# Moving sixteen element-wise sums and products of a mixture-of-experts stage from GpSimd to VectorE

## The chip, the cores and the metric

The kernel runs on one core of a Trainium2 chip. A core has five engines that work at once and tell each other of finished work through semaphores: TensorE (PE in the profile; its weight loads are listed as PEld), VectorE (DVE), ScalarE (ACT), GpSimd (POOL) and SyncE (SP), which in this kernel issues most DMAs. GpSimd also issues the indirect DMAs (gathers and scatters by a list of rows). The metric is the device time of one execution in microseconds (us); of several runs the median is taken.

## The reference, cut to what matters

There is one block of a transformer with four batches of 512 tokens of width 256. First comes attention with 16 heads, then a mixture of eight experts of which every token uses two. Both halves are normalized, modulated by a small vector per batch, and added back through a gate.

```python
h = _layernorm(x) * (1 + ca) + sa
x = x + ga * attention(h)                      # 16 heads of 128, causal
h = _layernorm(x) * (1 + cb) + sb
down   = h @ down_w + down_b                   # 256 -> 128
probs  = softmax(h @ router_w + router_b - cost)
top 2 of 8 experts, gate = softmax(of the two probabilities)
out    = sum over the two experts e of gate * (gelu(gelu(down) @ w1[e] + b1[e]) @ w2[e] + b2[e])
out   += 0.1 * (gelu(gelu(down) @ shared_w1 + shared_b1) @ shared_w2 + shared_b2)
y      = out @ up_w + up_b + gelu(h) @ core_w + core_b
x      = x + gb * y
```

Everything is float32. The experts have hidden widths of 128 to 512.

## The kernel before, in words

**Layout.** Tokens stand on the 128 partitions; a batch is four tiles of 128 tokens by 256 columns (`xs[b]`, in the trace `x`). Two neighbouring tiles are handled as one operand of 128 x 512.

**Attention stage.** A loop over 64 heads, four heads of one batch at a time, runs from the start to about 630 us of the span. Three heads are still on their way when it ends; their last products are made between the first steps of the next stage. When four heads of a batch are summed in PSUM (`po`), `project_out` multiplies by the gate on VectorE (L626, `tmp`) and adds to `x` (the call of `on_pool` in its last lines).

**Mixture stage** (`all_ffn`, from about 620 us to the end). For each batch, in this order:

- `second_norm` normalizes, makes the modulated rows, and calls `down` (L665 on TensorE, L673 and L674 on VectorE), `route` (a run of small VectorE instructions, L696 to L741, which finds the two experts of each token and their gates) and `to_rows`.
- `to_rows` calls `place` (L814 and L817 on TensorE from the tile `mine`, L825 to L841 on VectorE: the row of each token in a table sorted by expert) and `bring` (L857: eight indirect DMAs on GpSimd that scatter the tokens into `table`).
- `Experts.get` (L963) loads the sorted rows through SyncE, `turn` (L973) transposes them on VectorE (`full_s`). `Chunks` then runs 20 chunks of 128 hidden units per batch: first product (L1025, `ph_s`), activation on ScalarE (L1033, `hid_s`), second product three chunks later (L983, `acc_s`). After each pair of experts VectorE takes the sum out (L993, `y_s`) and SyncE stores it in `given` (L1001).
- `take` (trace line L594, tile `taken`): eight indirect DMAs on GpSimd that gather each token's two expert rows from `given`. `gated` weighs the two (L1086 on ScalarE, L1087 on VectorE).
- `core` (L1156), `combine` (L1105 and L1113 on TensorE, L1122 on ScalarE) and `up` (L1170) make the output; `up` multiplies by the gate on VectorE (L1178) and adds `x`. The last three batches do this after all chunks; the first does it among the chunks of the third.
- `gate_bias`, once per batch: `gbias`, the two output biases' sum times the gate (128 x 256), is added to both halves of `x`. This is done ahead of the output.

**What sets the order.** In this stage TensorE, VectorE, ScalarE and SyncE run their instructions in the order in which the program emits them. `PLAN` says at which of the 80 chunks each side step is emitted. GpSimd is left to the scheduler, except that `on_pool` ties every GpSimd instruction behind the one before (`pool_order`), so that its instructions keep the order of emission too. Each engine's queue is served strictly in turn: an instruction that waits holds back all that stand behind it on its engine. All calls through `on_pool` show as L594 in the profile.

GpSimd's queue in the mixture stage, in order: scatter of batch 1; two adds into `x` of batch 3 (last heads); `gbias` of batches 0 and 1 and their four adds; two small steps of batch 3's norm; scatter of batch 2; gather of batch 0; scatter of batch 3; two adds of batch 0's outputs; `gbias` of batch 2 and its first add; two DMAs of batch 1's gather; second add of batch 2; the other six DMAs; `gbias` of batch 3 and its two adds; gather of batch 2; gather of batch 3.

Of the kernel before, what the change touches and what calls it, by code (L numbers as in the profile page):

```python
# [16 lines left out]
ALU = mybir.AluOpType  # L17
# [94 lines left out]
def adaln_attention_moe_kernel(  # L112
# [14 lines left out]
    nc = tc.nc  # L127
# [476 lines left out]
    def project_out(b: int, h: int, z):  # L604


        g, j = h // HG, h % HG
        if j == 0:
            outs[b, g] = [
                psum.tile([P, 2, D], F32, tag=f"po{u}", name=f"po_{b}_{g}_{u}", bufs=1)  # L610
                for u in range(NT // 2)
            ]
        for u, po in enumerate(outs[b, g]):
            for t in range(2):
                tok = ts(2 * u + t, P)

                mm3(
                    po[:, t, :],
                    (z[0][:, tok], z[1][:, tok]),
                    part(wo_u[h // 2], (h % 2) * D, D),  # L620
                    j == 0 and t == 0,
                    j == HG - 1 and t == 1,
                )
            if j == HG - 1:
                tmp = work.tile([P, 2, D], F32, tag="tmp", name=f"tmp_{b}_{g}_{u}")
                nc.vector.tensor_tensor(tmp, po, pair(gate_a[b]), ALU.mult)  # L626
                xu = xs[b][:, 2 * u : 2 * u + 2, :]
                on_pool(nc.gpsimd.tensor_tensor, xu, xu, tmp, ALU.add)

# [506 lines left out]
    def gate_bias(b: int):  # L1138

        gbias = work.tile([P, D], F32, tag="vf", name=f"gbias_{b}", bufs=3)  # L1140
        on_pool(nc.gpsimd.tensor_tensor, gbias, rest_state["obias"], gate_b[b], ALU.mult)
        yield
        for u in range(NT // 2):
            xu = xs[b][:, 2 * u : 2 * u + 2, :]
            on_pool(nc.gpsimd.tensor_tensor, xu, xu, pair(gbias), ALU.add)
            yield

    pys: dict[tuple[int, int], bass.AP] = {}
# [15 lines left out]
    def up(b: int, u: int, last: bool = False, also: str = ""):  # L1164
        py = pys[b, u]
        y = work.tile([P, 2, D], F32, tag="tmp", name=f"y_{b}_{u}{also}")
        xu = xs[b][:, 2 * u : 2 * u + 2, :]
# [8 lines left out]
            )  # L1176
        if not last:
            nc.vector.tensor_tensor(y, py, pair(gate_b[b]), ALU.mult)  # L1178
            if also or b == 0:
                on_pool(nc.gpsimd.tensor_tensor, y, y, xu, ALU.add)  # L1180
            else:
                nc.vector.tensor_tensor(y, y, xu, ALU.add)
            stores.append((out[r0 : r0 + 2 * P, :].rearrange("(t p) d -> p t d", p=P), y))
            return
        for t in range(2):
# [553 lines left out]
```

## Time and profile before

| | us |
|---|---|
| median of 5 runs | 796.26 |
| lowest and highest | 792.53, 797.79 |
| the profiled execution | 796.48 |
| its span, first to last instruction | 794.8 |
| TensorE busy | 750.8 (94%) |
| VectorE busy | 541.0 (68%) |
| GpSimd busy | 470.4 (59%) |
| mean granted TensorE clock | 0.973 |

In a timeline each line has the start, the duration, the engine, the program's line, the operation, the tile written `<-` the tiles read, the shapes, and a count; brackets hold the idle time of the engine just before it and what ended this idle time. "remote" or "another core or an unknown queue" means that the profile can't name what ended it, and "issue" that it shows no wait that ended then. In a table by stage each row has the stretch of the span, its length, each engine's busy time with its instructions in brackets, the granted TensorE clock, the share of the DMA engines, and GB/s. The end of a matmul is modelled and not measured.

The sixteen instructions that the change touches take this time on GpSimd: eight adds of `gbias` to `x`, 10.1 us; four products `gbias`, 2.9 us; two adds of batch 0's outputs, 2.5 us; two adds of the last heads, 2.5 us.

### The profile page before, as it was taken

What the parts mean: (1) busy time and instruction counts of PE and PEld (TensorE: products, weight loads), DVE (VectorE), ACT (ScalarE), POOL (GpSimd) and SP (SyncE); (2) the same over time, 40 slices, a digit from 0 to 9 for tenths busy, and PEclk for the clock granted to TensorE, in tenths of its full rate; (3) what the DMA queues carried; (4) which work ended last, traced back from release to release, by engine and by line L of the source; (5) the groups of instructions that cost most, each with busy time, mean ns of one, the idle gap of its engine ahead of it and who ended that gap; (6) DMA issues with size and microseconds to landing.
All of it is one profiled execution on the core that took longest, in us unless ns stands there. A gap on an engine that the chain in (4) does not pass through costs nothing.

```text
span 794.8 us, 14400 instructions
## 1 busy us (share of the span) xinstructions
PE 750.8 (94%) x4641; PEld 679.0 (85%) x4641; DVE 541.0 (68%) x1753; ACT 470.8 (59%) x1180; POOL 470.4 (59%) x497
## 2 busy tenths in 40 slices
PE   8999999999999999999999999998998989478895
PEld 8899999999999999999999999997987879467784
DVE  6897887777777777777767777777785766133323
ACT  4668676776666677666667766665664436144430
POOL 4467657676655668675657786665467255634640
PEclk9999999999999999999999999999999999798997
DMA  7455455665566678776667756543567524352522
GB/s 254 134 178 193 128 166 147 178 200 147 143 177 186 166 212 227 209 189 184 180 166 197 216 152 179 161 141 112 152 188 187 129 54 100 73 113 72 125 87 73
DMA packets 111554, 124.68 MB, mean 157 GB/s; under 512 B 42592, under 2 KB 96624, under 8 KB 111472
## 3 DMA queue, kind: packets, MB, share of 16 engines
q1 hardware_dynamic: 109008, 119.47, 54.4%
q0 software_dynamic: 2048, 4.20, 1.8%
q8 instruction: 39, 0.64, 0.3%
q14 instruction: 43, 0.35, 0.1%
q10 hardware_dynamic: 416, 0.02, 0.0%
HBM read 64.92 MB, written 58.73 MB: 156 GB/s over the span
## 4 chain that ended last, share of the span: by engine, by line
PE 84%; DVE 7%; issue 3%; POOL 2%; another core or an unknown queue 1%; ACT 1%; DMA 1%; SPq 0%; DVEq 0%; ACTq 0%
PE ph_s L1025 4%; PE ps L139 4%; PE ps L138 4%; PE pz L139 4%; PE pz L140 4%; PE ps L140 4%; PE pz L138 4%; PE acc_s L983 4%; PE pv L140 4%; PE pv L139 4%; PE pv L138 4%; PE po L138 3%; PE po L140 3%; PE pk L139 3%; PE po L139 3%; PE pk L140 3%
## 5 line engine op out<-in xcount | busy, mean ns | idle before, releaser
L522 POOL TENSOR_SCALAR e<-e,inv 128x128 f32<-128x128 f32 (+3 forms) x256 | 137.4, 544 | 206.1 <-DVE inv L521 195.7
L517 ACT ACTIVATE e<-e,nmax 128x128 f32<-128x128 f32 (+3 forms) x256 | 144.0, 565 | 75.6 <-DVE nmax L507 73.9
L146 POOL TENSOR_TENSOR aT<-aT,aTh 128x1152 fp32r<-128x1152 f32 x61 | 163.5, 2680 | 10.8 <-ACT aTh L554 3.2
L507 DVE CUSTOM_DVE_ANT_0 e<-ps,mask 128x128 f32<-128x128 f32 (+3 forms) x256 | 123.3, 487 | 63.4 <-PE ps L140 39.7
L537 DVE STREAM_TRANSPOSE T<-e 128x384 f32<-128x384 f32 (+2 forms) x256 | 100.8, 447 | 35.3 <-POOL e L522 35.3
L575 ACT CAST zh<-pz 128x512 fp32r<-128x512 f32 x64 | 37.6, 588 | 90.7 <-PE pz L571 90.7
L554 ACT CAST aTh<-aT 128x1152 fp32r<-128x1152 f32 x64 | 73.1, 1143 | 3.4 <-DMA aT<-moved 3.3
L138 PE MATMUL po<-wo,zl 128*128 128x256 f32 x256 | 72.7, 284 | 1.7 <-DVE zl L146 1.7
L138 PE MATMUL ps<-kh,ql 128*128 128x256 f32 (+2 forms) x192 | 71.3, 371 | 3.0 <-DVE nmax L507 3.0
L140 PE MATMUL pv<-wv,hTh 128*128 128x256 f32 x256 | 72.6, 284 | 0.0
L139 PE MATMUL pv<-wv,hTh 128*128 128x256 f32 x256 | 72.5, 283 | 0.0
L139 PE MATMUL po<-wo,zh 128*128 128x256 f32 x256 | 72.2, 282 | 0.0
L138 PE MATMUL pv<-wv,hTl 128*128 128x256 f32 x256 | 72.1, 281 | 0.0
L140 PE MATMUL po<-wo,zh 128*128 128x256 f32 x256 | 72.0, 281 | 0.0
L1033 ACT ACTIVATE hid_s<-ph_s,cols 128x256 f32<-128x256 f32 x80 | 37.0, 473 | 55.2 <-PE ph_s L1025 28.6
L139 PE MATMUL pz<-aT,vh 128*128 128x512 f32 (+2 forms) x192 | 65.5, 341 | 2.8 <-POOL aT L146 1.9
L140 PE MATMUL pz<-aTh,vh 128*128 128x512 f32 (+2 forms) x192 | 65.9, 343 | 0.0
L138 PE MATMUL pz<-aTh,vl 128*128 128x512 f32 (+2 forms) x192 | 65.6, 342 | 0.0
L139 PE MATMUL ps<-kl,qh 128*128 128x256 f32 (+2 forms) x192 | 65.4, 340 | 0.1
L140 PE MATMUL ps<-kh,qh 128*128 128x256 f32 (+2 forms) x192 | 64.9, 338 | 0.0
L521 DVE RECIPROCAL inv<-tot 128x1 f32<-128x1 f32 x256 | 39.9, 159 | 32.6 <-ACT e L517 27.6
L1025 PE MATMUL ph_s<-full_s,wf_first 128*128 128x256 f32 x128 | 41.3, 407 | 13.6 <-issue 9.0
(223 smaller groups left out, 2112.0 us busy)
## 6 DMA issues: line engine op xcount, KB each, us to landing
moved<-T SPq DMA_DIRECT2D x256, 160.0 KB
aT<-moved SPq DMA_DIRECT2D x64, 640.0 KB
st_wqk<-in_wqk SPq DMA_DIRECT2D x16, 256.0 KB
got_s<-table SPq DMA_DIRECT2D x64, 64.0 KB
given<-y_s SPq DMA_DIRECT2D x16, 256.0 KB
table<-mask SPq DMA_DIRECT2D x8, 384.0 KB
given<-mask SPq DMA_DIRECT2D x8, 384.0 KB
st_wv<-in_wv SPq DMA_DIRECT2D x8, 256.0 KB
```

The source lines that it names most:

```text
L138: nc.tensor.matmul(o, lhsT=wl, rhs=mh, start=start, stop=False)
L139: nc.tensor.matmul(o, lhsT=wh, rhs=ml, start=False, stop=False)
L140: nc.tensor.matmul(o, lhsT=wh, rhs=mh, start=False, stop=stop)
L146: return eng.tensor_tensor(lo, full, f32(hi), ALU.subtract)
L507: least = nc.vector.tensor_tensor_reduce(out=et, in0=ps[:, :n], in1=maskf[:, S - n :], scale=-SCALE, scalar=BIG, op0=ALU.add, op1=ALU.min, ...
L517: exp = nc.scalar.activation(et, et, AF.Exp, bias=nm[:, t : t + 1], scale=-1.0, accum_out=tot[:, t : t + 1])
L521: nc.vector.reciprocal(inv[:, one], tot[:, one])
L522: by_sum = nc.gpsimd.tensor_scalar(et, et, inv[:, one], 1.0, ALU.mult, ALU.mult)
L537: nc.vector.transpose(to[:, first : first + n], blocks[:, at : at + (n - 1) * step + 1 : step])
L554: nc.scalar.copy(hi, full)
L575: recent["z"] = nc.scalar.copy(zh.rearrange(by_block, a=NB, r=R), pz).ins
L1025: nc.tensor.matmul(ph, lhsT=w1(k), rhs=m.ready[i][:, half * PLACES : (half + 1) * PLACES], start=True, stop=True,)
```

## The change

Sixteen instructions of the mixture stage change engine: the two adds after the last heads, the four products and eight adds of `gate_bias`, and the two adds of the first batch's outputs. They go into VectorE's program order at the places where they are emitted. With `in_order` set, which is so in the mixture stage alone, `project_out` adds on VectorE; during the attention loop it adds on GpSimd as before. The operands, the shapes and the arithmetic stay.

```diff
@@ project_out
-                on_pool(nc.gpsimd.tensor_tensor, xu, xu, tmp, ALU.add)
+                if in_order:
+                    nc.vector.tensor_tensor(xu, xu, tmp, ALU.add)
+                else:
+                    nc.gpsimd.tensor_tensor(xu, xu, tmp, ALU.add)
@@ gate_bias
-        on_pool(nc.gpsimd.tensor_tensor, gbias, rest_state["obias"], gate_b[b], ALU.mult)
+        nc.vector.tensor_tensor(gbias, rest_state["obias"], gate_b[b], ALU.mult)
         yield
         for u in range(NT // 2):
             xu = xs[b][:, 2 * u : 2 * u + 2, :]
-            on_pool(nc.gpsimd.tensor_tensor, xu, xu, pair(gbias), ALU.add)
+            nc.vector.tensor_tensor(xu, xu, pair(gbias), ALU.add)
             yield
@@ up
             nc.vector.tensor_tensor(y, py, pair(gate_b[b]), ALU.mult)
-            if also or b == 0:
-                on_pool(nc.gpsimd.tensor_tensor, y, y, xu, ALU.add)
-            else:
-                nc.vector.tensor_tensor(y, y, xu, ALU.add)
+            nc.vector.tensor_tensor(y, y, xu, ALU.add)
```

On VectorE the sixteen stand here: the adds of the last heads each behind its own product (L626); `gbias` of batches 0 and 1 behind `dtok` of batch 2 (L674), the four adds in pairs within the routing of batch 2, ahead of `mine`; the adds of batch 0's outputs each behind its product (L1178); `gbias` and adds of batch 2 around the first two transposes and the first `y_s` that follow; those of batch 3 around the transpose behind batch 1's weighing. The order of all other instructions on VectorE, and all of TensorE's, ScalarE's and SyncE's order, stays the same. On GpSimd the scatters and gathers now stand next to each other: scatter 2, gather 0, scatter 3, gather 1, gather 2, gather 3, with nothing between them.

## The prediction

> **What bounds the kernel now.** First I read the page: TensorE is busy nearly throughout, and its granted clock (tenths, last line) is nearly full until the last fifth of the span.
>
> ```profile
> span 794.8 us, 14400 instructions
> PE 750.8 (94%) x4641; PEld 679.0 (85%) x4641; DVE 541.0 (68%) x1753; ACT 470.8 (59%) x1180; POOL 470.4 (59%) x497
> ...
> PEclk9999999999999999999999999999999999798997
> ```
>
> Hence the question is what the change does to TensorE in the mixture stage. The table by stage cuts that stage by GpSimd's work. Its columns are the stretch, its length, each engine's busy time, then the granted clock.
>
> ```profile
> core 0: us, PE busy (x) PEld busy (x) DVE busy (x) ACT busy (x) POOL busy (x), PEclk, DMA share, GB/s
> ...
> 652.00:671.70 19.70, 19.29 (x136) 17.78 (x137) 15.27 (x54) 11.73 (x26) 8.65 (x10) 1.00 0.52 107
> 671.70:694.00 22.30, 11.70 (x76) 10.69 (x75) 5.16 (x21) 4.98 (x12) 15.45 (x16) 0.78 0.36 83
> ...
> 703.80:716.00 12.20, 6.62 (x39) 5.81 (x38) 3.16 (x11) 3.37 (x10) 7.74 (x8) 0.95 0.53 119
> ...
> 729.20:741.60 12.40, 10.64 (x73) 9.86 (x72) 3.50 (x10) 6.13 (x16) 10.25 (x11) 1.00 0.81 189
> ...
> 747.50:759.00 11.50, 9.52 (x54) 8.62 (x52) 2.69 (x4) 2.86 (x7) 7.61 (x8) 0.85 0.54 123
> ```
>
> Between the runs of indirect DMAs TensorE has no hole (19.29 of 19.70 us). Beside them it has: 10.6 us are missing from 671.70 to 694.00 (scatter 2 and gather 0), 5.6 from 703.80 to 716.00 (scatter 3), 1.8 beside gather 1, 2.0 beside gather 2, and the clock falls as well. TensorE's timeline has the holes in brackets:
>
> ```profile
> 684.36 1.19 PE L1025 MATMUL ph_s<-full_s,wf_first 128*128 128x256 f32 x2 [3.53 <-DVE dtok L674]
> 693.48 1.22 PE L1025 MATMUL ph_s<-full_s,wf_first 128*128 128x256 f32 x2 [7.07 <-issue]
> ...
> 709.70 0.60 PE L801 MATMUL ptk<-ident,dtok 128*128 128x128 f32 x4
> 715.88 2.08 PE L1105 MATMUL po_sum<-act_shared,wf_core 128*128 128x512 f32 x2 [5.58 <-ACT dF L803]
> ...
> 722.22 1.03 PE L1170 MATMUL py<-wf_core,sum 128*128 128x256 f32 x4
> ...
> 751.10 0.67 PE L1025 MATMUL ph_s<-full_s,wf_first 128*128 128x256 f32 x2 [1.98 <-issue]
> ```
>
> ScalarE's timeline says why:
>
> ```profile
> 692.95 0.47 ACT L1033 ACTIVATE hid_s<-ph_s,cols 128x256 f32<-128x256 f32 x1 [9.34 <-remote]
> ...
> 715.24 0.59 ACT L803 COPY dF<-ptk 128x512 f32<-128x512 f32 x1 [5.22 <-remote]
> 719.70 0.69 ACT L1122 ACTIVATE sum<-po_sum,cvec 128x512 f32<-128x512 f32 x1 [3.87 <-PE po_sum L1113]
> ```
>
> The transpose `ptk` of 709.70 is over at 710.30, yet the copy that needs only it starts at 715.24, released by something the profile can't name; TensorE's `po_sum` waits for that copy. Without indirect DMAs the same step is immediate: `po_sum` ends at 719.66, `sum` starts at 719.70. So while GpSimd issues indirect DMAs, TensorE's results reach the other engines late, and TensorE runs dry. Read against GpSimd's timeline, the releases come again 1.5 us after scatter 3's last DMA (713.74) and 1.2 to 2.7 us after gather 0's (691.72).
>
> ```profile
> 690.77 0.95 POOL L594 DMA_INDIRECT taken<-given,places  x1 [0.30 <-issue]
> ...
> 712.78 0.96 POOL L857 DMA_INDIRECT table<-dtok,places  x1 [0.30 <-issue]
> 724.07 1.27 POOL L594 TENSOR_TENSOR y<-y,x 128x512 f32<-128x512 f32 x1 [10.32 <-DVE g L710]
> ...
> 729.26 1.00 POOL L594 DMA_INDIRECT taken<-given,places  x1 [0.15 <-issue]
> ```
>
> These lines carry the forecast. GpSimd is free from 713.74, but its next instruction in order, the add of batch 0's outputs, waits until 724.07 for `up`; gather 1 stands behind it and behind a product and an add, and starts at 729.26. SyncE issues batch 1's last store at 707.14. For batch 2 store and gather lie 3.2 us apart (744.38 and 747.58), so gather 1's data are there near 710.3.
>
> **The change, part by part.** Against the profiled execution (span 794.8 us, 1.7 around it, 796.48 in all, 0.2 above the median).
>
> *Removed from GpSimd.* Twelve sums at 1.27 us (L594 rows) and four products at 0.73 make 18.2 us. GpSimd is busy 59% and is not on the path by its own work. Directly this gives nothing.
>
> *Added to VectorE.* Twelve sums at 0.69 (L1182, same shape, both operands in SBUF) and four products at 0.42 make 10.0 us. By place:
>
> - Last heads: two sums behind L626, where VectorE idles 2.00 us and 1.45 us before its next instruction. Nothing; without those idles, 1.4 us.
> - Batches 0 and 1: two products and four sums, ahead of `mine` of batch 2.
>
> ```profile
> 660.80 0.69 DVE L993 TENSOR_TENSOR y_s<-acc_s,idle 128x512 f32<-128x512 f32 x1 [0.69 <-PE acc_s L983]
> ...
> 665.69 0.19 DVE L720 TENSOR_TENSOR mine<-hot 128x32 f32<-128x32 f32 x1
> ```
>
> The products (0.84) fit in the 0.69 before `y_s`, as L697 loses the 0.24 by which it was longer beside GpSimd's sums (0.43 against 0.19). The four sums add 2.7, L699 gives back 0.3 for the same reason: `mine` is 2.3 to 2.4 later. TensorE comes to `place` at 666.95, 1.1 after `mine` ends, and its queue stops there for some 1.2 us. The norm of batch 3 stands in the same row: its reciprocal root on GpSimd is done 1.4 us after L354, so `xn` goes from 668.27 to 669.8, and TensorE's transposes behind it with it. Scatter 2 moves alike. I take **+1.5 us**; ends: +0.7 (2.7 less both slacks, 1.1 and the 0.98 of VectorE before `y_s` at 667.15) and +2.8 (no slack left).
> - Batch 0's outputs, `gbias` 2: VectorE idles 0.98 us between them and 1.03 behind. The transposes there come 1.1 later; the first ended at 726.34 and is needed at 728.32. Nothing; 1.1 without that slack. The new wait of `gbias` 2 is for gate rows that SyncE issues at 709.92; in VectorE's queue `y_s` and two transposes stand behind it, but those rows are 17 us old by then.
> - Batch 3's product and sums: the 5.0 us that VectorE waits before 750.25 cover the sums. The product is counted below.
>
> *Gather 1 moves.* On GpSimd nothing stands between scatter 3 and gather 1 any more: gather 1 starts at 714.0 and ends at 724.0 (eight steps of 1.25). That makes 20 us of indirect DMAs without a break, as scatter 2 and gather 0 are now. What this costs no row shows for this place. Above: with the copy of `ptk` held to 725.5, TensorE's restart goes from 715.88 to 726.1, +10.2. Below: gather 1 where it is now leaves the releases prompt for its first 8 us and costs TensorE 0.23; taking that, 0. Nearest is scatter 2 with gather 0, where two releases got through at 683.1, 1.4 us after the last scatter, and hardly any until gather 0 ended. So `ptk` gets through near 715.2, TensorE makes `po_sum` and two chunks, and stops at 722.2 before L1170, as `sum` waits for `po_sum`. That release comes 1.5 us after the gather, at 725.5; 0.7 for `sum` and 0.5 to restart make 726.7: +4.5. Then the clock. After the 5.58 us hole TensorE had half its clock for 6.8 us; a second hole of 4.5 us gives perhaps 4.4 us of it, +2.2. I take **+6.7 us**, ends 0 and +10.2.
>
> *Gather 1 no longer stands at 729 to 740.* There it made L1087 late (VectorE waits 2.29, 1.78 and 1.15 us for `taken`), behind it `y_s` at 743.67, the store, and the loads on SyncE that `full_s` at 750.25 waits for. TensorE's holes from this: 0.23, 0.35, 1.98. Less 0.42 for the product ahead of the transpose: 2.1. The granted clock was 0.51 from 752.2 to 755.6 behind the last hole; undone, this gives 1.7. I take **-3.8 us**, ends 0 and -4.3. The 1.76 us hole at 735.51 stays: all engines read a flag there.
>
> Sum: 1.5 + 6.7 - 3.8 = +4.4, hence 796.48 + 4.4 = 800.9 us. The tail (from 761 us) is TensorE's own work and only shifts.
>
> **Two rules of the Trainium skill against these rows.** The 1.98 us hole was followed by half the clock for 3.4 us. The Trainium skill, "TensorE: Matmul & The Clock Gate", section "What's actually happening", asks for a whole idle window of about 3.4 us before the clock halves; then the 1.7 us would not come back, and the sum would be +6.1 (802.6). The row shows it after less, and decides.
> The releases 5 us late beside indirect DMAs are a row too. The Trainium skill, "SBUF — State Buffer", section "Who interferes with whom", says that DMAs never contend with a compute engine and that TensorE and ScalarE wait on no one. By it the moved gather would cost nothing: -2.3 (794.2). The trace speaks against using it here, whatever path the releases take.
>
> **The rivals.**
> *The gather holds everything* (20%): `ptk` itself is stuck until the gather's end. 1.5 + 10.2 - 3.8 = +7.9: 804.4. For it: of the releases pending after 683.1 none came for 7 us. Against: the two that came through at 683.1.
> *The early gather is harmless* (25%, not slower): TensorE's results get out beside a gather as they do beside gather 1 now. 1.5 + 0 - 3.8 = -2.3: 794.2. It decides when the moved gather costs under 2.3 us. For it: in gathers 1 and 2 the releases stay prompt for 8 us. Against: gather 0, which directly followed a scatter, is the same arrangement, and TensorE lost 7.07 us in it.
> *Gather 1 stays* (10%): something else holds it near 729, so only VectorE's part counts: +1.5, 798.0. Against: its data are there at 710.3.
>
> **How the numbers follow.** The first account has 45% and its own range of 797 to 804: 800.9. Rivals: 804.4, 794.2, 798.0. To leave out at most 2 in 10 the range goes from 793 (the harmless gather with VectorE's low end) to 806. A measurement of this kernel tells about 0.5% (4.0 us) from no change. Slower by more: 26 of the first's 45 points, 20 of the second's and some of the rest, 0.50. Faster by more: part of the harmless case, 0.11. Within: 0.39.
>
> **What would show it.** In GpSimd's timeline: gather 1 right behind scatter 3. In TensorE's: a hole of about 4.5 us at L1170 ahead of 727, a low clock behind it, none of the holes from 742 to 751; a wait of about 1 us at `place` near 667. In VectorE's: `mine` 2.3 us later. The forecast is wrong if `sum` follows `po_sum` at once beside gather 1, or if the first run (scatter 2 with gather 0) changes its own 10.6 us, which I hold fixed: it only shifts by 1.5.

## The result, and the profile after

The changed kernel's median is 797.65 us (52 runs, 792.4 to 802.1), against 795.23 us before (94 runs, 790.2 to 800.6): a ratio of 1.003, 95% interval 1.0019 to 1.0040, so 2.4 us slower. The forecast was 4.4 us slower. The experiments then showed a second thing that the forecast had no room for: there are runs in which the kernel before takes 775 us and not 795 us, and in those the same change is 0.8% faster. First the profile that answers to the one shown before. The profiled execution took 803.3 us, above the slowest of the 52 runs; the two profiled executions of this kernel in later 795 us runs took 806.7 and 802.3 us. So all three traces of it show executions 4 to 9 us above the median, and none shows what a run at the median looks like.

The page of the changed kernel, its span and its engines' busy times:

```profile
span 801.6 us, 14391 instructions
PE 752.6 (94%) x4641; PEld 681.0 (85%) x4641; DVE 548.1 (68%) x1769; ACT 470.8 (59%) x1180; POOL 450.9 (56%) x481
```

GpSimd lost its 16 instructions and 19.5 us, VectorE has 16 more and 7.1 us more. TensorE's timeline after, cut to the lines with its main holes, which stand in brackets (line numbers are 3 higher than before from the last heads' sums on):

```profile
652.83 1.09 PE L395 MATMUL ptn<-ident,xn 128*128 128x128 f32 x4 [2.15 <-ACT act_shared L1064]
670.06 0.38 PE L817 MATMUL pp<-mine,tri 128*128 128x32 f32 x2 [1.00 <-DVE mine L723]
690.59 1.22 PE L1028 MATMUL ph_s<-full_s,wf_first 128*128 128x256 f32 x2 [6.46 <-issue]
698.27 1.22 PE L1028 MATMUL ph_s<-full_s,wf_first 128*128 128x256 f32 x2 [5.61 <-ACT hid_s L1036]
...
721.98 2.07 PE L1108 MATMUL po_sum<-act_shared,wf_core 128*128 128x512 f32 x2 [6.21 <-issue]
731.25 1.96 PE L1173 MATMUL py<-wf_core,sum 128*128 128x256 f32 x4 [2.59 <-ACT sum L1125]
746.32 0.67 PE L1028 MATMUL ph_s<-full_s,wf_mixed 128*128 128x256 f32 x2 [1.76 <-DVE flag L1350]
759.54 0.67 PE L1028 MATMUL ph_s<-full_s,wf_first 128*128 128x256 f32 x2 [0.69 <-issue]
766.34 0.70 PE L1028 MATMUL ph_s<-full_s,wf_mixed 128*128 128x256 f32 x2 [1.03 <-issue]
```

New are the 1.00 us at `place` (it waits for `mine`, as forecast) and the 2.59 us at L1173 (forecast 4.5, at this place). Gone are the holes of 0.23, 0.35 and 1.98 us behind the flag read; 0.69 is left. New as well is 1.03 us at 766.34, at the end of gather 2, at a chunk that waited for nothing before. Larger are the first run's holes, 12.07 us in place of 10.60, and the wait of the last norm's transposes, 2.15 in place of 1.43.

ScalarE's and GpSimd's timelines show the chain behind L1173:

```profile
721.35 0.58 ACT L806 COPY dF<-ptk 128x512 f32<-128x512 f32 x1 [5.92 <-remote]
730.51 0.69 ACT L1125 ACTIVATE sum<-po_sum,cvec 128x512 f32<-128x512 f32 x1 [8.58 <-remote]
```

```profile
718.24 0.96 POOL L860 DMA_INDIRECT table<-dtok,places  x1 [0.30 <-issue]
719.51 0.97 POOL L594 DMA_INDIRECT taken<-given,places  x1 [0.30 <-issue]
...
728.30 0.95 POOL L594 DMA_INDIRECT taken<-given,places  x1 [0.31 <-issue]
```

Gather 1 now stands right behind scatter 3, with no gap but the usual 0.30 us, and ends at 729.25. TensorE's `po_sum` is over at 725.8 by the model, but `sum`, which needs only it, starts at 730.51, 1.3 us behind the gather's last DMA. In the profile before, `sum` followed `po_sum` within 0.04 us.

The table by stage (stretch, length, busy times, then the granted clock) shows what the clock added:

```profile
core 0: us, PE busy (x) PEld busy (x) DVE busy (x) ACT busy (x) POOL busy (x), PEclk, DMA share, GB/s
652.30:655.90 3.60, 3.07 (x12) 2.80 (x13) 3.52 (x8) 2.15 (x5) 0.00 (x0) 0.58 0.85 166
...
727.00:735.00 8.00, 5.41 (x21) 4.51 (x20) 1.46 (x3) 2.51 (x5) 1.90 (x2) 0.72 0.09 25
```

Behind the 2.15 us hole the clock is 0.58 for 3.6 us (3.6 x 0.42 = 1.5 us of work lost). Around the hole at L1173 it is 0.72 for 8 us; behind the hole itself it is half speed for 3.4 us, 1.7 us lost.

How much later each TensorE instruction starts than in the profile before gives the sum by place, waits and clock together: +0.3 us ahead of the last norm, +1.6 at it, +1.4 at `place`, +2.2 in the first run (half speed for 17.1 us, before 13.6), +5.3 at `po_sum` and L1173, -4.0 from there to 756 us (the relief; times of the profile before), +1.5 from 756 to 761 (the new hole at the end of gather 2), and -1.5 in the tail, where half the clock sets in at 786.4 us before and at 799.7 after. That is 6.8 us, as between the two spans. The medians differ by 2.4 us only, so a part of this is the choice of execution; the experiments say of some parts which.

### The profile page after: what moved, and what is told of

Read it like the earlier page. It is cut to its first block, busy times and chain, and to the rows that moved or that the text cites. A ratio compares the mean times of both kernels' runs of the same rounds, so it can differ in the third digit from the quotient of the medians.

```text
span 801.6 us, 14391 instructions
## 1 busy us (share of the span) xinstructions
PE 752.6 (94%) x4641; PEld 681.0 (85%) x4641; DVE 548.1 (68%) x1769; ACT 470.8 (59%) x1180; POOL 450.9 (56%) x481
## 4 chain that ended last, share of the span: by engine, by line
PE 83%; DVE 5%; another core or an unknown queue 4%; DMA 2%; issue 2%; ACT 2%; POOL 1%; SPq 0%; ACTq 0%; DVEq 0%
PE ph_s L1028 4%; PE pz L139 4%; PE ps L139 4%; PE pz L140 4%; PE ps L138 4%; PE pz L138 4%; PE ps L140 4%; PE acc_s L986 4%; PE pv L140 4%; PE pv L139 4%; PE pv L138 3%; PE po L138 3%; PE pk L138 3%; PE pk L139 3%; PE pq L138 3%
## 5 line engine op out<-in xcount | busy, mean ns | idle before, releaser
L594 POOL DMA_INDIRECT taken<-given,places x32 | 30.8, 962 | 45.1 <-DMA got_s<-table 26.6
```

## The experiments

The runs come in five sets. Within a set all kernels and the kernel before ran on one chip; ratios are always to the kernel before of that set. In sets 1, 2 and 4 that kernel took 796.6, 794.8 and 795.7 us, in sets 3 and 5 776.7 and 773.6 us. I call them the 795 us sets and the 775 us sets (the expectations speak of chips of the 795 us and the 777 us kind). Set 1 and set 5 carry the same chip number, so it isn't the chip alone.

### The parts, one at a time (795 us sets)

The first batch's output sums alone on VectorE (the kernel before, third edit only):

```diff
@@ up
-            if also or b == 0:
-                on_pool(nc.gpsimd.tensor_tensor, y, y, xu, ALU.add)
-            else:
-                nc.vector.tensor_tensor(y, y, xu, ALU.add)
+            nc.vector.tensor_tensor(y, y, xu, ALU.add)
```

> The kernel before with one part done alone: only the two sums of batch 0's outputs go to VectorE. Gather 1 then waits only for the product and one sum of batch 2 on GpSimd and starts near 716, some 13 us earlier; the routing of batch 2 on VectorE is untouched. Theory: +6.7 for the hole and the clock, -3.8 for the relief: +1 to +3 us, ratio 1.001 to 1.004, with a hole at the first L1170 and no hole at place. Rival A (early gather harmless): only the relief, -2 to -4 us, ratio 0.995 to 0.998.

Measured: 797.17 us, ratio 1.0006 (0.9987 to 1.0026). No hole at L1170: behind scatter 3 came the product and one sum of batch 2's bias (715.37 to 717.43), then two DMAs of gather 1, the other sum, and the other six DMAs from 721.3. So gather 1 stood early here, but not back to back with the scatter, and the hole that was expected didn't come.

The gated biases of batches 0 and 1 alone on VectorE:

```diff
@@ gate_bias
+        def on(*args):
+            if b < 2:
+                nc.vector.tensor_tensor(*args)
+            else:
+                on_pool(nc.gpsimd.tensor_tensor, *args)
-        on_pool(nc.gpsimd.tensor_tensor, gbias, rest_state["obias"], gate_b[b], ALU.mult)
+        on(gbias, rest_state["obias"], gate_b[b], ALU.mult)
```

(and its sums likewise)

> The kernel before with one part done alone: gate_bias of batches 0 and 1 goes to VectorE, everything else stays on GpSimd; gather 1 stays where it was. Theory: a hole of about 1 us at place near 667 and all behind it 1.5 us later, ratio 1.001 to 1.003. Rival (the runs of indirect DMAs behind it swallow the delay, as TensorE waits in them anyway): 1.000. Rival A (the whole loss of the changed kernel is here): ratio 1.003 or more.

Measured: 797.34 us, ratio 1.0015 (0.9990 to 1.0039). The wait at `place` is 1.00 us, as in the changed kernel, so this is the part that makes it.

The last heads' sums alone on VectorE:

```diff
@@ project_out
-                on_pool(nc.gpsimd.tensor_tensor, xu, xu, tmp, ALU.add)
+                if in_order:
+                    nc.vector.tensor_tensor(xu, xu, tmp, ALU.add)
+                else:
+                    on_pool(nc.gpsimd.tensor_tensor, xu, xu, tmp, ALU.add)
```

> The kernel before, with only the last heads' two output sums on VectorE. The prediction costed these at nothing. Theory now, from the trace of the changed kernel (TensorE waits 2.15 us at the transposes of the last norm where it waited 1.43 us, and has half its clock for 3.4 us behind): +0.7 us of waiting and +1.6 of clock, ratio about 1.003. Rival, the prediction's own term: the sums lie in VectorE's idle time, the wait stays at 1.4 us, ratio 1.000. Either way no hole at L1173 (gather 1 still stands behind the output sums on GpSimd), and no hole at place.

Measured: 797.29 us, ratio 1.0025 (0.9997 to 1.0053), which holds both 1.000 and 1.003. The wait at the transposes was 2.14 us, without a half clock behind it. A later profile of the unchanged kernel (before_look, below) has 2.12 us there too, so the 0.7 us can't be put down to these sums. Along TensorE this trace has lost 0.7 us to the first profile behind the wait, and nothing from 658 us on. By the time this part stays undecided between 0 and 4 us; the trace shows no cost.

The last heads' sums and the biases of batches 0 and 1 together, which leaves gather 1 where it was:

> The kernel before, with the last heads' sums and the biases of batches 0 and 1 on VectorE; the biases of batches 2 and 3 and batch 0's outputs stay on GpSimd, so gather 1 stays where it was before. On a chip of the 795 us kind: the wait at place (1.0 us) and the last heads' part (0.7 us, in some executions 1.7 of clock), ratio 1.002 to 1.004, the same as the whole change. On a chip of the 777 us kind: no VectorE instruction held for 5 us beside GpSimd's sums, so the whole gain of the change there, ratio 0.990 to 0.995. Rival there (the gain comes from gather 1's place or from batch 0's outputs): 1.000.

Measured in a 795 us set: 797.28 us, ratio 1.0012 (0.9983 to 1.0041). The wait at `place` is 0.99 us, there is no hole at L1173. As this run fell in a 795 us set, these eight instructions alone have no measurement at 775 us. In the same set the whole change, a second time:

> The changed kernel on the chip of this call. On a chip of the 795 us kind 1.003 (1.001 to 1.005); on one of the 777 us kind 0.992 (0.989 to 0.996). Rival (the two measurements differ by chance and not by the chip): a ratio between them, near 0.998, on either kind.

Measured: 798.43 us, ratio 1.0032 (1.0008 to 1.0056); it repeats the first measurement. Its holes: 2.16 at the transposes, 1.00 at `place`, 12.10 in the first run, 5.53 at `po_sum`, 3.79 at L1173. And one execution of it in set 1:

> The changed kernel once more, for a second trace. Theory: a hole near 1 us at place and one of 2 to 5 us at the first L1173 again, gather 1 right behind scatter 3, no hole over 1 us between the flag and the last chunk. If the sizes differ much from the first trace (1.00 and 2.59 us), the terms are not fixed from run to run and the forecast's single values could not hold.

Measured: 806.7 us in this one execution; 0.99 at `place`, 12.16, 5.60, and 3.95 us at L1173, with half the clock for 3.4 us behind it. Three executions of the changed kernel thus have 2.59, 3.95 and 3.79 us at L1173, and in the 795 us sets no kernel without gather 1 right behind scatter 3 has that hole.

### Where gather 1 stands (795 us sets)

The changed kernel with batch 0's output sums back on GpSimd, which puts gather 1 behind them again:

```diff
@@ up, in the changed kernel
-            nc.vector.tensor_tensor(y, y, xu, ALU.add)
+            if b == 0:
+                on_pool(nc.gpsimd.tensor_tensor, y, y, xu, ALU.add)
+            else:
+                nc.vector.tensor_tensor(y, y, xu, ALU.add)
```

> The changed kernel with one part undone: the two sums of batch 0's outputs stay on GpSimd, so that gather 1 waits behind them again and starts near 726 instead of right behind scatter 3. Theory (the moved gather makes TensorE's releases late, a hole of some 3 us at L1173 and half the clock behind it, and takes the later holes away): only the VectorE part is left, +1.5 us against the kernel before, no hole at the first L1173, and the holes between 742 and 751 are back; ratio 1.001 to 1.002. Rival A (the early gather is harmless and the whole loss is the VectorE part ahead of mine): as slow as the changed kernel or slower, since the relief of 3.8 us is lost: ratio 1.003 to 1.006. Rival B (the early gather costs all there is): ratio 1.000.

Measured: 803.69 us, ratio 1.0094 (1.0069 to 1.0120), a clear miss: undoing a part made it worse. TensorE's timeline of this kernel says where:

```profile
743.65 1.19 PE L1028 MATMUL ph_s<-full_s,wf_mixed 128*128 128x256 f32 x2 [5.29 <-DVE flags L1352]
```

Its GpSimd and VectorE:

```profile
740.71 0.94 POOL L594 DMA_INDIRECT taken<-given,places  x1 [0.30 <-issue]
```

```profile
741.92 0.69 DVE L996 TENSOR_TENSOR y_s<-acc_s,idle 128x512 f32<-128x512 f32 x1 [5.47 <-remote]
```

The hole at L1173 is gone, but gather 1 now runs from 731.8 to 741.65 without a break, over the place where all engines read the flag, and `y_s` ahead of the flag starts 0.27 us behind its last DMA. That hole, 1.76 us in the kernels before and after, is 5.29 us, and the clock is half from 741.9 to 748.8. In the first profile gather 1 lies on the flag read too (729.26 to 740.20), but there a sum on GpSimd stands between its second and its third DMA:

```profile
731.54 1.29 POOL L594 TENSOR_TENSOR x<-x,gbias 128x512 f32<-128x512 f32 x1
```

So the flag's 1.76 us, which the prediction held fixed, isn't fixed beside a gather without a break.

The changed kernel with one tiny GpSimd instruction ahead of gather 1 that needs `sum` of batch 0:

```diff
@@ take
+        if b == 1 and in_order:
+            held = small.tile([P, 1], F32, tag="held", name="held", bufs=1)
+            on_pool(nc.gpsimd.tensor_scalar, held, sums[0][:, :1], 1.0, 1.0, ALU.mult, ALU.mult)
```

> The changed kernel, with one tiny GpSimd instruction ahead of gather 1 that reads the sum of batch 0, so that gather 1 can't start before that sum is made (about 724 us). Theory (gather 1 right behind scatter 3 keeps po_sum's release from ScalarE): no hole of TensorE at L1173, no second stretch of half clock behind it, gather 1 from about 724.5 to 734.5, clear of the flag read near 741. That is 2.6 to 4.0 us of waiting and 1.7 of clock less than the changed kernel, less what gather 1 costs in its new place (0 to 2): 793 to 796 us, ratio 0.996 to 1.000 against before. Rival (gather 1 costs the same wherever it stands): the loss reappears as holes in 724 to 742, ratio 1.003 or more.

Measured: 798.17 us, ratio 1.0029 (0.9999 to 1.0060). In its profile the hole at L1173 is gone, gather 1 starts at 729.0, the flag's hole is 1.84, and from the first `ph_s` to the end it takes 169.4 us (628.8 to 798.2) where the changed kernel's first profile has 176.0. But the median doesn't show it: nine of its twelve runs lie at 796.5 to 801.1 and three at 792 to 793.1. The profiled execution (799.95) is one of the nine, and lost its time ahead of the mixture stage: in the other profiles at 795 us the first `ph_s` starts at 622.1 to 626.4 us. What the other eight lost isn't shown. As a measurement of the median this run is inconclusive.

Gather 1 as plain DMAs on SyncE's queue:

```diff
@@ take, in the changed kernel
+            if b == 1 and not also:
+                for k in range(2):
+                    nc.sync.dma_start(y[:, k, t, :], given[b][(k * NT + t) * P :][:P, :])
+                yield
+                continue
```

> The changed kernel, with gather 1 as eight plain DMAs of the same size on SyncE's queue, each of 128 rows that follow one another (the wrong rows for the tokens: the outputs of batch 1 are not the reference's). The same bytes move, but GpSimd issues no indirect DMA for them. Theory (it is GpSimd's indirect DMAs that hold TensorE's releases): sum follows po_sum at once, no hole at L1173 even with the bytes moving at the same time, and the relief from 742 to 751 stays: about 4 us less than the changed kernel, ratio 0.997 to 0.999. Rival (the transfer itself, its bytes or its packets, holds them): the hole of 2.6 to 4.0 us stays, ratio about 1.003.

Measured: 793.71 us, ratio 0.9988 (0.9963 to 1.0013), against 1.0030 for the changed kernel: 0.0042 x 795 = 3.3 us less, with some 2 us of uncertainty (the two intervals' half widths, 0.0025 and 0.0010). `sum` follows `po_sum` at once. Its profile also has less loss ahead of gather 1 (10.66 us of holes in the first run and half the clock for 13.7 us, and no half clock at the last norm), so the 3.3 us aren't all the gather's. And SyncE issued these DMAs only at 727 to 735, so the bytes did not move beside `po_sum`, and the rival, that the transfer itself holds the releases, was not put to the test by this run. The next ones do that.

### Breaks between the indirect DMAs

The changed kernel with a GpSimd instruction on one column ahead of every pair of gather DMAs. All indirect DMAs and all their bytes stay.

```diff
@@ take, in the changed kernel (Chunks.first leaves its newest hidden tile in pace[0])
         for t in range(NT):
+            if b < 3 and not also:
+                held = small.tile([P, 1], F32, tag="held", name=f"held_{b}_{t}", bufs=1)
+                on_pool(nc.gpsimd.tensor_scalar, held, pace[0][:, :1], 1.0, 1.0, ALU.mult, ALU.mult)
             for k in range(2):
```

> The changed kernel, with a tiny GpSimd instruction ahead of each pair of gather DMAs of batches 0 to 2 that reads the hidden tile which ScalarE made last, so that the pairs go with the chunks of the mixture and not back to back. Theory (back-to-back indirect DMAs hold TensorE's releases, a pause lets them through): of the 12 us lost beside scatter 2 and gather 0, 3 to 5 come back; no hole at L1173 (2.6 to 4.0, and 1.7 of clock); 787 to 792 us, ratio 0.989 to 0.996. Rival (each indirect DMA has its own cost, wherever it stands): the same sum of holes, spread, ratio about 1.003. Second rival (the pauses themselves stall ScalarE, as the hidden tile can't be written again before GpSimd has read it): waits of ScalarE for GpSimd ahead of hid_s, ratio over 1.006.

Measured: 789.72 us (6 runs, 782.1 to 797.3), ratio 0.9898 (0.9847 to 0.9949). The first run's holes fall from 12.1 to 3.61 + 2.54 = 6.15 us, the one at L1173 is gone, `po_sum` keeps 5.28 (scatter 3 isn't paced). In the first run all indirect DMAs and all bytes are still there, so half of its holes don't come from their number or bytes, but from how they stand. At L1173 the run says less: the first of the inserted instructions waited 12.47 us for its hidden tile, so gather 1 started only at 725.01. Then the scatters of batches 2 and 3 as well, whose pairs are now also emitted one step after another:

```diff
@@ bring
         for t in range(NT):
-            if t == NT // 2 and not in_order:
+            if (t == NT // 2 and not in_order) or (in_order and t and pace):
                 yield
+            if in_order and t and pace:
+                held = small.tile([P, 1], F32, tag="held", name=f"sheld_{b}_{t}", bufs=1)
+                on_pool(nc.gpsimd.tensor_scalar, held, pace[0][:, :1], 1.0, 1.0, ALU.mult, ALU.mult)
```

> The changed kernel with scatters 2 and 3 and the gathers paced, on another chip if this call has one. On a chip of the 795 us kind: the holes beside scatter 2 with gather 0 (12 us) and at po_sum (5.3 us) shrink to under 5 us together, 778 to 786 us, ratio 0.978 to 0.988; if the rows come too late instead, waits for full_s and 0.990 or above. On a chip of the 777 us kind: 0.992, the same as the changed kernel.

Measured in a 795 us set: 782.54 us, ratio 0.9830 (0.9798 to 0.9863), the best of all versions there. TensorE's, ScalarE's and GpSimd's timelines of this kernel:

```profile
702.66 0.60 PE L804 MATMUL ptk<-ident,dtok 128*128 128x128 f32 x4
703.93 1.13 PE L1116 MATMUL po_sum<-act_shared,wf_core 128*128 128x512 f32 x2 [0.67 <-issue]
```

```profile
703.30 0.59 ACT L806 COPY dF<-ptk 128x512 f32<-128x512 f32 x1 [0.41 <-issue]
```

```profile
701.51 0.96 POOL L863 DMA_INDIRECT table<-dtok,places  x1 [0.30 <-issue]
702.50 0.20 POOL L594 TENSOR_SCALAR sheld<-hid_s 128x1 f32<-128x1 f32 x1
702.87 1.00 POOL L863 DMA_INDIRECT table<-dtok,places  x1 [0.17 <-issue]
704.18 0.96 POOL L863 DMA_INDIRECT table<-dtok,places  x1 [0.31 <-issue]
```

In the middle of scatter 3 the copy of `ptk` now starts 0.04 us after the transposes' end, where it waited 4.9 us in the kernel before, and `po_sum` waits 0.67 us and not 5.58. The first run's holes are 1.56 + 3.18 + 1.21 = 5.95 us. The inserted instruction takes 0.2 us and mostly waits for nothing, so it hardly slows the DMAs down: an instruction of another sort between two pairs is enough here. Two things aren't shown: whether any instruction would do, as this one also reads ScalarE's newest tile; and what the copy had waited for, as the profile calls it "remote". That it was the notice of TensorE's result is an inference, from the 775 us sets below, where `ptk` releases the same copy at once.

### The other runs: 775 us

Set 3 was meant to take the costs apart further, and found other conditions. The first four expectations, each with its kernel: the kernel before with batch 0's output sums and the biases of batches 2 and 3 on VectorE (run again further below), the kernel before with paced gathers, the changed kernel with everything paced, and the changed kernel.

> The kernel before, with only what moves gather 1 to right behind scatter 3: batch 0's output sums and the biases of batches 2 and 3 on VectorE. The last heads' sums and the biases of batches 0 and 1 stay on GpSimd. The prediction's terms for this are B +6.7 and C -3.8, so +2.9 us, ratio 1.0036, with a hole of 4.5 us at the first py<-wf_core,sum. Theory after the runs so far (the hole is 2.6 to 4.0 us with 1.7 of clock behind it, and about 4 us come back from 742 on): 0 to +2, ratio 1.000 to 1.0025; no wait at place for mine, 1.4 us at the last norm's transposes. Rival (the loss of the whole change is all gather 1's): 1.003.

> The kernel before (all 16 moved instructions on GpSimd again), with the paced gathers of the run gathers_paced. Theory: with the gathers paced, gather 1's place no longer matters, and what is left of the change is the wait at place (1.0 us) and the last heads' (0.7 us, and 1.7 of clock): 2 to 3 us less than gathers_paced, ratio 0.985 to 0.988. Rival (the change's other costs are nothing, or GpSimd's own sums delay the gathers as much): the same as gathers_paced, 0.990, or above it.

> The run gathers_paced with scatters 2 and 3 paced too: a tiny GpSimd instruction that reads the newest hidden tile ahead of every pair of their DMAs but the first. Theory (releases are held beside back-to-back indirect DMAs): the 5.3 us hole at po_sum and the 3.6 us hole beside scatter 2 shrink to under 2 us each, and the half clock behind them is shorter; 3 to 6 us less than gathers_paced, ratio 0.982 to 0.987. Rival (the rows reach the table later, and the loads of batch 2's and 3's rows with them): TensorE waits for full_s instead, 0.990 or above.

> The changed kernel once more, beside the three others on one chip. 1.003 (1.001 to 1.005) against before by the first measurement; a second look at its holes: 2.15 us at the last norm's transposes, 1.0 at place, 12 beside scatter 2 and gather 0, 5.6 at po_sum, 2.6 to 4.0 at py<-wf_core,sum.

| run | median us | ratio (95%) |
|---|---|---|
| gather1_early_alone | 778.09 | 0.9999 (0.9954 to 1.0045) |
| before_paced | 774.45 | 1.0009 (0.9971 to 1.0046) |
| all_paced | 770.32 | 0.9922 (0.9890 to 0.9954) |
| changed_same_chip | 771.06 | 0.9923 (0.9889 to 0.9956) |

All expectations that were built on late releases fell. TensorE's, ScalarE's and GpSimd's timelines of changed_same_chip, at the place where the first profile of the changed kernel has its holes of 6.21 and 2.59 us:

```profile
697.44 1.12 PE L1108 MATMUL po_sum<-act_shared,wf_core 128*128 128x512 f32 x2 [0.68 <-ACT dF L806]
```

```profile
696.80 0.58 ACT L806 COPY dF<-ptk 128x512 f32<-128x512 f32 x1 [0.41 <-PE ptk L804]
699.49 0.69 ACT L1125 ACTIVATE sum<-po_sum,cvec 128x512 f32<-128x512 f32 x1 [2.11 <-DMA got_s<-table]
```

```profile
695.19 0.95 POOL L860 DMA_INDIRECT table<-dtok,places  x1 [0.31 <-issue]
696.45 0.96 POOL L860 DMA_INDIRECT table<-dtok,places  x1 [0.30 <-issue]
697.71 0.95 POOL L860 DMA_INDIRECT table<-dtok,places  x1 [0.30 <-issue]
698.97 0.98 POOL L594 DMA_INDIRECT taken<-given,places  x1 [0.30 <-PE po_sum L1116]
```

The same 16 indirect DMAs go out back to back, at the same 0.95 and 0.30 us, and TensorE's releases arrive at once. The longest hole of this profile's mixture stage is 2.50 us. In these sets neither gather 1's place nor pacing is worth anything that the table could tell from nothing (its intervals reach 0.3 to 0.5% to each side).

One sign goes with the sets in all twenty traces: in the fourteen at 795 us the list of DMAs gives no time from issue to landing for any kind of DMA, in the six at 775 us it gives one for 26 to 37 of the 37 kinds. The same line for the kernel before, from a 795 us and a 775 us execution (the last figure is the median in us):

```profile
got_s<-table SPq DMA_DIRECT2D x64, 64.0 KB
```

```profile
got_s<-table SPq DMA_DIRECT2D x64, 64.0 KB, 2.6
```

So a trace tells which kind it is. Why the records of landings are missing, and whether that has to do with the late releases, isn't shown.

But then why is the change faster by 0.8% (6.0 us by the ratio, 5.7 by the medians)? It isn't gather 1's part (gather1_early_alone: 0.9999), so by elimination it is the eight other instructions near 650 us. A profile of the kernel before in set 5:

> The kernel before, for a profile on the chip of this call. On a chip of the 777 us kind: a VectorE instruction of 0.15 us held for about 5 us beside GpSimd's sums near 650 us, and TensorE waiting 2 to 7 us at ph_s behind it. On one of the 795 us kind: the holes of the first profile.

It took 773.26 us. VectorE's and GpSimd's timelines:

```profile
650.71 1.94 DVE L921 TENSOR_REDUCE idle_row<-idle 128x128 f32<-128x1024 f32 x1 [1.97 <-POOL x L594]
652.57 0.16 DVE L710 SCALAR_TENSOR_TENSOR g<-g,r_g 128x4 f32<-128x4 f32 x1
652.63 0.71 DVE L973 STREAM_TRANSPOSE full_s<-got_s 128x512 f32<-128x512 f32 x1
653.26 4.99 DVE L733 SCALAR_TENSOR_TENSOR g<-g,r_sm 128x4 f32<-128x4 f32 x1
658.17 0.68 DVE L993 TENSOR_TENSOR y_s<-acc_s,idle 128x512 f32<-128x512 f32 x1
```

```profile
649.39 2.51 POOL L594 TENSOR_TENSOR x<-x,tmp 128x512 f32<-128x512 f32 x2
651.86 1.46 POOL L594 TENSOR_TENSOR gbias<-obias,gate 128x256 f32<-128x256 f32 x2
653.28 4.94 POOL L594 TENSOR_TENSOR x<-x,gbias 128x512 f32<-128x512 f32 x4
```

L733 works on four columns and took 0.12 us in the first profile. Here it lasts 4.99 us, until GpSimd's four sums are over (658.22), with all of VectorE's queue behind it. TensorE waits 1.08 us behind it, and 1.65 us before that behind the transpose, which stood behind L921 and its 1.97 us wait for a GpSimd sum. In the changed kernel neither wait is there: from this profile to that of changed_same_chip TensorE gains 2.9 us between 652 and 661 us, and loses 1.2 at `place`. In gather1_early_alone, which has the same sums on GpSimd, another instruction of the same kind was caught, and it stands ahead of the transpose that TensorE needs. VectorE's and TensorE's timelines of that kernel:

```profile
651.13 5.58 DVE L710 SCALAR_TENSOR_TENSOR g<-g,r_g 128x4 f32<-128x4 f32 x1
656.63 0.70 DVE L973 STREAM_TRANSPOSE full_s<-got_s 128x512 f32<-128x512 f32 x1
```

```profile
658.04 1.22 PE L1025 MATMUL ph_s<-full_s,wf_first 128*128 128x256 f32 x2 [7.09 <-ACT full_s L975]
```

7.09 us of waiting, with half the clock from 654.9 to 661.7 around it, in an execution of 777.46 us. Which of the two is caught differs between executions of one kernel: the second time gather1_early_alone was run, L733 was caught, for 4.97 us, in an execution of 770.67 us.

> The run gather1_early_alone on another chip, if this call has one. On a chip of the 795 us kind the prediction's terms B +6.7 and C -3.8 say +2.9, ratio 1.0036, and the holes measured in the traces of the changed kernel (2.6 to 4.0 us at py<-wf_core,sum, 1.7 of clock, about 4 us back from 742 on) say 0 to +2, ratio 1.000 to 1.0025. Rival (what the whole change costs there, 1.003, is all from gather 1): 1.003. On a chip of the 777 us kind 1.000 again.

Measured: 776.24 us, ratio 0.9999 (0.9956 to 1.0041), as the first time. (It too fell in a 775 us set, so gather 1's part alone has no measurement at 795 us.) This fits the wide spread of the kernel before, though the two profiles alone don't show that it makes it: its 35 runs in set 3 lie from 768.8 to 783.1 us, while the changed kernel and all_paced, which have no sums on GpSimd, stay within 768.9 to 772.7 and 766.9 to 772.0.

Last, the kernel before, unchanged, in set 4:

> The kernel before, for a profile of it on the chip of this call. If the chip is like that of the last four runs (776.7 us before), the account is: TensorE has no holes beside indirect DMAs, but where GpSimd makes the last heads' and the first gated biases' sums (8 sums and products without a break, near 648 to 657 us) a VectorE instruction of 0.15 us on four columns lasts 5 us, the transpose full_s behind it is late, and TensorE waits 2 to 7 us at ph_s; none of that in the changed kernel. If the chip is like the earlier ones (795 us): holes as in the first profile, ratio 1.000 either way.

Measured: 793.61 us, ratio 0.9986 (0.9959 to 1.0013), so two measurements of one kernel differ by this much. Its holes: 2.12 at the last norm's transposes, 4.99 + 5.66 in the first run, 4.12 at `po_sum`, 1.69 at 746 and 1.37 at 753. VectorE's timeline has the held instructions here too, for the length of one sum:

```profile
657.76 1.14 DVE L697 TENSOR_TENSOR r_lg<-r_lg,r_m 128x32 f32<-128x32 f32 x1
...
660.18 1.18 DVE L699 SCALAR_TENSOR_TENSOR r_s<-r_lg,desc 128x32 f32<-128x32 f32 x1
```

In the first profile the same two took 0.43 and 0.47 us. At 795 us GpSimd's sums start later (`gbias` at 656.08 in the first profile, after 3.06 us of waiting), when the transpose `full_s` is over, and VectorE waits for TensorE's `pd` anyway.

## Why the prediction was right or wrong

**The sign and the range: right where the forecast was made; the size too large.** At 795 us the change costs 2.4 to 2.5 us in two measurements (1.0030 and 1.0032), against 4.4 forecast. At 775 us it gains 6.0, outside the forecast's range.

**"I take +1.5 us" for VectorE's sums ahead of `mine`: right.** The wait at `place` is 0.99 or 1.00 us in every kernel that has the biases of batches 0 and 1 on VectorE, and none without them; forecast 1.2. Clock and waits together, TensorE is 1.35 us later behind `place` in each of the three traces of the changed kernel, against +1.5. The part alone measured +1.2 us (1.0015), with an interval from -0.8 to 3.1.

**"Gather 1 moves. I take +6.7 us": the step that failed at 795 us, by its size.** The hole stands at the place named, with gather 1 right behind scatter 3, and it goes when a break or another place is given to the gather. It measured 2.59, 3.95 and 3.79 us against 4.5, and the clock 1.7 against 2.2; along TensorE `po_sum` and L1173 together cost 5.3, 4.7 and 4.6 us. The prediction took the release too late: `sum` started 1.3, 0.7 and 0.5 us behind the gather's last DMA and not 1.5, and TensorE restarted 0.74 us after `sum` began and not 1.2. In the first of the three `ptk` also got through 0.6 us later than forecast. So the term is 1.4 to 2.1 us too large, and the whole sum 2.0. That the one makes the other is not shown: the three traces come to +5.8 to +10.1 us, with costs in them that the prediction put at nothing, and no run at 795 us measures the gather's move alone. What a median run of the changed kernel doesn't pay stays open. The rival that the gather holds everything (+10.2) and the one that it is harmless (0) both fall in the traces at 795 us; at 775 us the harmless one is what happens.

**"I take -3.8 us" for gather 1 gone from 729 to 740: right up to 756 us, then lost again in part or wholly.** TensorE regains 4.0, 4.0 and 4.1 us between 735 and 756 in the three traces. But by 761 it loses 1.5, 5.4 and 2.4 us again, in new holes at the end of gather 2 that the first profile doesn't have, so -2.5, +1.4 and -1.7 are left. The second profile of the unchanged kernel regains 2.6 us there against the first and loses 1.6 again, so even a part of this is the choice of execution. With the term above, gather 1's move nets +2.8, +6.1 and +2.9 us, against +2.9 forecast: two terms that were each too large cancel in two of the three, which is luck.

**"The first run keeps its 10.6 us": wrong in the traces, its cause open.** The changed kernel has 12.07, 12.16 and 12.10 us there and 17.1 us of half clock, the kernel before 10.60 and 10.65 with 13.6. But y_adds_alone, which is the kernel before up to that point, has 12.14, and gather1_plain, which has the change, 10.66. Two levels exist. Of the eight unpaced traces at 795 us with the biases of batches 0 and 1 on VectorE seven are on the upper one, of the four without one is: that the change favours it is suggested, not shown. The prediction had named this as a sign of being wrong, and its term for it was nothing.

**The clock rule: the row was the better guide, but not a rule.** The prediction took half clock behind a hole of 2 us from one row, against the Trainium skill, "TensorE: Matmul & The Clock Gate", section "What's actually happening", which asks for a whole idle window of about 3.4 us. The changed kernel has it behind 2.15 us (0.58 over 3.6 us), and y_adds_alone behind 1.43 us, after a stretch of 3.4 us in which TensorE was busy for 1.51. Three other executions have holes of 2.1 us without it, and before_look one of 1.69, where the prediction's row had 1.98.

**Last heads' sums "Nothing": undecided**, 0 to 4 us by the run, though its trace shows no cost. The 1.6 us at the last norm in the trace of the changed kernel are the half clock there, which also comes without these sums (y_adds_alone) and stays away with them (last_heads_alone, gather1_plain).

**"Directly this gives nothing" for the 18 us taken off GpSimd: the step that failed at 775 us.** The prediction saw the two VectorE instructions that lasted 0.43 and 0.47 us beside GpSimd's sums, and wrote the 0.24 us off as a small return. What such an instruction loses depends on how it falls against the sums: the same kind was longer by 0.24, 1.0, 4.9 and 5.4 us, the last with a 7.09 us hole of TensorE behind it. What removing the sums is worth should have been weighed against GpSimd's unbroken stretch of sums and products (8.8 us, 649.39 to 658.22), not by the excess that one execution happened to show. That this is the whole 6.0 us is argued, by elimination and from four traces; no run moved these eight instructions alone at 775 us. The Trainium skill, "SBUF — State Buffer", section "Who interferes with whom", says that a VectorE instruction with two inputs in SBUF and a GpSimd instruction that reads SBUF contend for a port that the one to start first holds for its whole instruction. The rows agree that the VectorE instruction is blocked, and show more: L733 was held over four sums in a row and not one.

**The premise of the late releases holds at 795 us alone.** The prediction read it off one execution as a property of the arrangement. The 775 us sets have the same arrangement, the same DMAs and no delay. The same section of that page, by which a DMA never contends with a compute engine and TensorE and ScalarE wait on no one, fits those sets. It speaks of ports of SBUF, and no run shows that the late releases of the 795 us sets come from a port; they show only that the rule can't be read as "GpSimd's DMAs cost TensorE nothing", as the prediction did where it worked out -2.3 us by it. What differs between the sets stays open.

## What to carry to other kernels

Where one engine issues a long row of indirect DMAs, look at when other engines go on behind each other's results, not only at what the DMAs move; a tiny instruction between every two pairs was worth 2.0% over the changed kernel in a 795 us set (798.43 to 782.54 us), far more than the change studied, and nothing in a 775 us set. Price the removal of work from GpSimd by the VectorE instructions that stand beside it and could be held, at the length of GpSimd's unbroken stretch; "it is idle 40% of the time" is no bound. And take a second profile of the kernel before and a second chip before believing a term of a few microseconds: hole sizes in one execution differed by 1 to 2 us from those of the next, the stage ahead by up to 7 us, and a change had opposite signs in two sets of runs.

## What the runs showed that was not expected

- The same kernel takes 795 us in some sets and 775 us in others. The difference lies in the mixture stage, mostly in TensorE's holes beside back-to-back indirect DMAs and in half clock: from the first `ph_s` to the end the kernel before takes 170.0 us (624.8 to 794.8) in one and 147.7 (623.8 to 771.5) in the other, while the attention stage ahead of it is the same within 1 us. Over all profiles the first `ph_s` starts at 621.9 to 625.9 us at 775 us and at 622.1 to 628.8 us at 795 us, so the stage ahead adds some us of its own to any single execution.
- In the 795 us sets a GpSimd compute instruction of 0.2 us between pairs of indirect DMAs lets the held results through: the copy of `ptk` waited 4.9 us without and 0.04 us with it. Why isn't shown.
- A VectorE instruction on 128 x 4 elements lasted 4.99 us, the length of four sums on GpSimd. In before_look one on 128 x 32 was held for 1.14 us and got its turn within such a row of four. What decides this isn't shown.
- Half the clock followed the holes of 2.6 to 4.0 us at L1173 for 3.4 us each time. Of the holes of 2.1 us at the last norm's transposes some were followed by it (the changed kernel, three times of three at 795 us) and some not (last_heads_alone, before_look, gather1_plain, which has the change).
